# Where ScalarE's two last exponentials stand among the copies of the transposed weights

## Chip, cores and metric

The kernel runs on one core of a Trainium2 chip. The metric is the device time of one execution in microseconds (us). The core has a matrix engine (TensorE, PE in the profile, with its weight loads listed apart as PEld), VectorE (DVE), ScalarE (ACT), GpSimd (POOL) and a queue engine (SP). Each engine works through its own list of instructions in order; semaphores order the engines against each other.

## What is computed

Two layers on x of 2 x 512 tokens x 256 features, all in float32. Layer 0 is a state-space scan and a mixture of eight experts. Layer 1 is causal attention with 32 query heads and 8 key/value heads of 64, gated by a network of signs. Only the attention of layer 1 matters here:

```python
q = (h @ Wq.T)...; k = (h @ Wk.T)...; v = (h @ Wv.T)...   # 32, 8 and 8 heads of 64
q, k = apply_rope(q), apply_rope(k)
logits = einsum('bhqd,bhkd->bhqk', q, k) * scale
logits = where(causal, logits, finfo.min)
attn = softmax(logits)
out = einsum('bhqk,bhkd->bhqd', attn, v)
return out.reshape(b, s, H * HD) @ Wo.T
```

## The kernel before

Everything ahead of the attention (layer 0 and the first projections of layer 1) is not touched. The attention is one hand-written order of work under a manual schedule: the loop `for n, (b, c) in enumerate(work)` has 32 iterations, n = 0 to 31, one for each pair of heads (16 pairs in each of two batches). The two heads of a pair are numbered hh = 0 and 1. The 512 queries are four tiles of 128, i = 0 to 3; because of the causal mask tile i meets (i + 1) x 128 keys, so that the last tile (`last`, i = 3) is 128x512.

The loop is staggered: iteration n scores pair n, and transposes and applies the weights of pair n - 1, which are finished by then. In iteration n each engine finds this order:

- TensorE: `scores` (L1213, 32 matmuls); the query projection of pair n + 1 (`projected`, L1145, 4 matmuls); 20 transposes of the weights of pair n - 1 (`transposed`, L1252) into six banks of PSUM, three for each head; in iterations 1 to 17 a piece of other work from a list (`others`: key and value projections, gates); then `values` (L1264, 16 matmuls), which multiplies the transposed weights with v.
- VectorE: `greatest` (L1226), which masks the scores, moves them from PSUM to the tile `pr` and finds the maximum `nmax`; in between `kept` (L1409, L1412), which stores the result of `values`; the rotation of the next query (L1135 to L1140) with the reciprocal of the sums of tiles 0 to 2 in its middle (L1428); then the reciprocal of the sums of tile 3 of both heads (`den3`, L1450) and the normalisation of tile 3 of head 0 (L1240).
- ScalarE: `exponentials` (L1232) of tiles 0 to 2, two heads each, in place in `pr`, with the row sum as a second result; then the six copies (L1253) that bring the transposed weights of pair n - 1 from PSUM to the tile `pt`, two of 128x512 and four of 128x384; the two exponentials of tile 3, 128x512 each; and the normalisation of tile 3 of head 1 (L1238).
- GpSimd: the normalisation of tiles 0 to 2 (L1240), six instructions.

The order on ScalarE between the copies and the last two exponentials is written out in the loop. `transposed(pts, pr, n)` does bank n of both heads: TensorE's transposes and ScalarE's two copies. Before, it is: bank 0, exponential of head 0, banks 1 and 2, exponential of head 1.

PSUM is eight banks handed out in turn (`bank`), `pt` has three buffers for the two of each iteration. `values` waits for each copy by itself: its matmuls go through key tiles j = 0 to 3, for j = 0 from the copies of bank 0, for j = 1 from bank 1, for j = 2 and 3 from bank 2. After iteration 31 the kernel sums the output projection (`summed`, L1272) for what is finished, transposes and copies pair 31 with no exponential among the copies, applies its values and ends.

Of the kernel before, what the change touches and what calls it, by code (L numbers as in the profile page):

```python
# [51 lines left out]
def fused_kernel(  # L52
# [41 lines left out]
    def bank(width=512):  # L94

        if not later:
            return bank_b()
        i = turns[0] % 8
        turns[0] += 1
        written[i] = max(written[i], width)  # L100
        return later[i]
# [1075 lines left out]
    def query(b, c, between=None):  # L1177
        q = aw.tile([P, T], F32, tag="q", name=f"q{b}_{c}")
        rotated(q, projected(w_q, c, b), 1.0, f"q{b}_{c}", between)
        return q  # L1180

    last = TPB - 1

    def scores(b, c, q):

        m = c // 4
        w = dict(  # L1190
            nmax=[aw.tile([P, TPB], F32, tag=f"nmax{hh}", name=f"nmax{b}_{c}_{hh}")
                  for hh in range(2)],

            den=aw.tile([P, 2, last], F32, tag="den0", name=f"den{b}_{c}_0"),
            den3=aw.tile([P, 2], F32, tag="den1", name=f"den{b}_{c}_1"),
            pr=[aw.tile([P, PACK], F32, tag=f"pr{hh}", name=f"pr{b}_{c}_{hh}")
                for hh in range(2)],
            ps={})
        for tiles in ((0, 1), (2,), (3,)):
            ready = written[turns[0] % 8], written[(turns[0] + 1) % 8]  # L1200
            pss = [bank(sum(i + 1 for i in tiles) * P) for _ in range(2)]
            for i in tiles:
                a = sum((k + 1) * P for k in tiles if k < i)
                cols = slice(a, a + (i + 1) * P)
                w["ps"][i] = [p[:, cols] for p in pss]
                for part in range(2):
                    to = slice(part * HD, (part + 1) * HD)
                    for hh in range(2):
                        half = slice(hh * HD, (hh + 1) * HD)
                        n = 2 * i + (part ^ (i & 1))  # L1210

                        full = (n + 1) * HD if ready[hh] >= cols.stop else (i + 1) * P
                        PE.matmul(pss[hh][to, a : a + full], lhsT=q[half, n * HD : (n + 1) * HD],  # L1213
                                  rhs=kT[b][half, m, :full], start=True, stop=True)
        return w

    def span(i):
        return slice(row_at[i], row_at[i] + (i + 1) * P)

    def sum_of(w, i, hh):  # L1220
        return w["den3"][:, hh : hh + 1] if i == last else w["den"][:, hh, i : i + 1]

    def greatest(w, i):

        for hh in range(2):
            V.tensor_tensor_reduce(w["pr"][hh][:, span(i)], w["ps"][i][hh],  # L1226
                                   cmask[:, i & 1, T - (i + 1) * P :], -1.0, 3.0e38, ALU.add, ALU.min,
                                   w["nmax"][hh][:, i : i + 1])

    def exponentials(w, i, hh):  # L1230
        x = w["pr"][hh][:, span(i)]
        S.activation(x, x, AF.Exp, scale=-1.0, bias=w["nmax"][hh][:, i : i + 1],  # L1232
                     accum_out=sum_of(w, i, hh))

    def normalised(w, i, hh, eng):
        x = w["pr"][hh][:, span(i)]
        if eng is S:
            S.mul(x, x, sum_of(w, i, hh))  # L1238
        else:
            eng.tensor_scalar(x, x, sum_of(w, i, hh), None, ALU.mult)  # L1240

    def transposes_begun(b, c):
        return [late.tile([P, PACK], F32, tag="pt", name=f"pt{b}_{c}_{hh}", bufs=3)
                for hh in range(2)]

    def transposed(pts, pr, n):
        for hh in range(2):
            ps = bank(widths[n])
            for (j, i), (bk, col) in place.items():
                if bk == n:  # L1250
                    at = row_at[i] + j * P
                    PE.transpose(ps[:, col : col + P], pr[hh][:, at : at + P], ident)  # L1252
            S.copy(pts[hh][:, bank_at[n] : bank_at[n] + widths[n]], ps[:, : widths[n]])  # L1253

    def values(b, c, pts):

        pv = bank()
        for j in range(TPB):
            bk, col = place[j, j]
            at = bank_at[bk] + col  # L1260
            w = T - j * P
            for hh in range(2):
                g = 2 * (c // 4) + hh
                PE.matmul(pv[hh * HD : (hh + 1) * HD, j * P :],  # L1264
                          lhsT=v_sb[b][:, j, g * HD : (g + 1) * HD],
                          rhs=pts[hh][:, at : at + w],
                          start=(j == 0), stop=(j == TPB - 1))
        return pv

    def summed(ps, b, i, pairs):  # L1270
        for c in pairs:
            PE.matmul(ps[:, :C], lhsT=oTs[b][:, c, i * P : (i + 1) * P],  # L1272
                      rhs=made["w_o"][c // 8][:, c % 8, :],
                      start=(c == 0), stop=(c == PAIRS - 1))
# [126 lines left out]
    def kept(b, c, pv):  # L1401
        if b not in oTs:
            oTs[b] = late.tile([P, PAIRS, T], F32, tag="oT", name=f"oT{b}")
        def halves(ap):
            return ap.rearrange("p (u s r q) -> p s r u q", s=2, r=2, q=HD)


        o, pv = oTs[b][:, c, :], pv[:, :]
        V.tensor_copy(o.rearrange("p (u s q) -> p s u q", s=2, q=P)[:, 0],  # L1409
                      pv.rearrange("p (u s q) -> p s u q", s=2, q=P)[:, 0])  # L1410
        for r in range(2):
            V.tensor_copy(halves(o)[:, 1, r], halves(pv)[:, 1, 1 - r])  # L1412

    with tc.manual_schedule():
        prev = done = None
        for n, (b, c) in enumerate(work):
            w = scores(b, c, nextq)
            for i in range(TPB):
                greatest(w, i)
                if i == 1 and done is not None:  # L1420
                    kept(*done)
                    done = None
                if i < last:
                    for hh in range(2):
                        exponentials(w, i, hh)

            def between():
                V.reciprocal(w["den"], w["den"])  # L1428

            if n + 1 < len(work):  # L1430
                nextq = query(*work[n + 1], between)
            else:
                between()
            for hh in range(2):
                for i in range(last):
                    normalised(w, i, hh, G)
            if prev is not None:
                pb, pc, pw = prev
                pts = transposes_begun(pb, pc)
                transposed(pts, pw["pr"], 0)  # L1440
                exponentials(w, last, 0)
                transposed(pts, pw["pr"], 1)
                transposed(pts, pw["pr"], 2)
                exponentials(w, last, 1)
            else:
                exponentials(w, last, 0)
                exponentials(w, last, 1)
            if others:
                others.pop(0)()
            V.reciprocal(w["den3"], w["den3"])  # L1450
            normalised(w, last, 0, V)
            normalised(w, last, 1, S)
            if prev is not None:
                done = (pb, pc, values(pb, pc, pts))
            prev = (b, c, w)
            if done is not None and done[1] == PAIRS - 1:
                kept(*done)
                done = None
                for i in range(TPB):
                    ps = bank(C)  # L1460
                    summed(ps, pb, i, range(PAIRS))
                    ended(ps, pb, i)

        kept(*done)
        pss = [bank(C) for _ in range(2)]
        for i in range(2):
            summed(pss[i], b, i, range(PAIRS - 1))
        pts = transposes_begun(b, c)
        for k in range(3):
            transposed(pts, w["pr"], k)  # L1470
        turns[0] += 2
        kept(b, c, values(b, c, pts))
        for i in range(2):
            summed(pss[i], b, i, range(PAIRS - 1, PAIRS))
            ended(pss[i], b, i)
        for i in range(2, TPB):
            ps = bank(C)
            summed(ps, b, i, range(PAIRS))
            ended(ps, b, i)
# [87 lines left out]
```

## Time and profile before

| what | value |
|---|---|
| median of the runs before | 644.58 us (three runs: 639.34, 644.58, 645.81) |
| the profiled execution, device time | 638.66 us |
| its span from the first to the last instruction | 636.9 us |
| TensorE's granted clock in it | 0.996 |
| busy: PE, DVE, ACT, POOL | 608.4, 430.3, 357.4, 276.8 us |
| the attention loop within the span | 256 to about 600 us |
| the output projection of batch 0 inside it | 440 to 468 us |
| iterations 19 to 30, from one to the next | 8.70 to 8.72 us |

All times inside the program come from the profiled execution and are counted from the first instruction of its span. "Idle before" an instruction is the time in which its engine did nothing ahead of it, and the arrow names what ended it. Matmuls overlap: a matmul's own duration in the profile is longer than the distance to the next one, so the time of a phase of matmuls is read from the first start to the last end, and a phase takes its first start to the next phase's first start of the engine.

### The profile page before, as it was taken

The page shows a single profiled execution, that of the slowest core. Times are in us where ns is not written, and L with a number is a line of the kernel's source. Part 1 is how long each engine was busy: PE and PEld are TensorE (multiplying, and loading weights), DVE is VectorE, ACT ScalarE, POOL GpSimd, SP SyncE. Part 2 cuts the span into 40 slices and gives each one's busy share as a digit, 9 for nine tenths or more (in the row PEclk, how much of TensorE's full clock was granted, in tenths as well). Part 3 has the DMA queues.
Part 4 walks back from the last instruction along what each step waited for, and adds up shares of the span by engine and source line. Part 5 has one row for each costly group of instructions (what it writes and reads, how often), then busy time and mean ns, then how long its engine had stood idle before and what let it go on. Part 6 is the DMA issues. An engine that isn't in the chain of part 4 may idle for free.

```text
span 636.9 us, 10937 instructions
## 1 busy us (share of the span) xinstructions
PE 608.4 (96%) x3818; PEld 411.2 (65%) x3818; DVE 430.3 (68%) x1375; ACT 357.4 (56%) x917; POOL 276.8 (43%) x309
## 2 busy tenths in 40 slices
PE   4999999999999998998899999899999999999997
PEld 2568888777577764454556565557866656666676
DVE  7587654564442257899989987996159888888411
ACT  2534333142331413868889877787058888898610
POOL 3021220264557312465566556365025776666600
PEclk9999999999999998999999999999999999999999
DMA  7710440555767344000000000040000000000000
GB/s 228 269 33 18 174 162 21 204 197 208 245 210 243 117 173 142 2 2 2 2 2 0 1 2 2 2 133 2 16 17 2 2 2 1 1 2 1 2 9 25
DMA packets 24988, 45.75 MB, mean 72 GB/s; under 512 B 2621, under 2 KB 12607, under 8 KB 24928
## 3 DMA queue, kind: packets, MB, share of 16 engines
q1 hardware_dynamic: 19024, 29.66, 13.5%
q0 software_dynamic: 4512, 13.77, 6.9%
q10 hardware_dynamic: 1392, 1.57, 0.7%
q8 instruction: 32, 0.52, 0.3%
q14 instruction: 28, 0.23, 0.1%
HBM read 40.80 MB, written 4.33 MB: 71 GB/s over the span
## 4 chain that ended last, share of the span: by engine, by line
PE 46%; DVE 14%; DMA 2%; issue 1%; POOL 1%; ACT 0%; ACTq 0%; DVEq 0%; POOLq 0%
PE bank L1264 9%; PE bank L1272 9%; PE bank L1252 8%; PE bank L1145 8%; PE bank L1213 8%; DVE pr L1226 5%; PE bank L1162 1%; DMA chosen<-o,dest 1%; PE bank L1124 1%; DVE sw_q L1135 1%; DVE xn L236 1%; DVE q L1136 1%; POOL pr L1240 1%; PE bank_b L1145 1%; DVE oT L1412 1%
## 5 line engine op out<-in xcount | busy, mean ns | idle before, releaser
L1240 POOL TENSOR_SCALAR pr<-pr,den 128x128 f32<-128x128 f32 (+2 forms) x192 | 193.1, 1021 | 154.2 <-DVE den L1428 121.0
L1232 ACT ACTIVATE pr<-pr,nmax 128x128 f32<-128x128 f32 (+3 forms) x256 | 142.7, 558 | 18.4 <-DVE nmax L1226 17.0
L1226 DVE CUSTOM_DVE_ANT_0 pr<-bank,cmask 128x128 f32<-128x128 f32 (+3 forms) x256 | 109.7, 484 | 14.5 <-PE bank L1213 11.9
L1253 ACT COPY pt<-bank 128x384 f32<-128x384 f32 (+1 forms) x192 | 84.8, 518 | 13.1 <-PE bank L1252 13.1
L1252 PEld LDWEIGHTS bank<-ident,pr 128*128 128x128 f32 x640 | 71.2, 141 | 24.7 <-issue 18.2
L1264 PE MATMUL bank<-pt,v 128*64 128x256 f32 (+3 forms) x512 | 82.5, 443 | 0.8 <-ACT pt L1253 0.8
L1252 PE MATMUL bank<-ident,pr 128*128 128x128 f32 x640 | 75.7, 273 | 6.0 <-DVE oT L1412 5.7
L633 PE MATMUL bank_a<-xgT,w 128*128 128x256 f32 x352 | 79.5, 379 | 0.0
L633 PEld LDWEIGHTS bank_a<-xgT,w 128*128 128x128 f32 x352 | 65.5, 190 | 9.2 <-issue 1.0
L1264 PEld LDWEIGHTS bank<-pt,v 128*64 128x64 f32 x512 | 39.3, 136 | 48.6 <-ACT pt L1253 22.3
L1213 PE MATMUL bank<-kT,q 64*64 64x128 f32 (+7 forms) x1024 | 69.8, 410 | 0.7 <-ACT v L1164 0.7
L1145 PE MATMUL bank<-x1T,w_q 128*128 128x512 f32 x124 | 61.5, 618 | 0.0
L1272 PE MATMUL bank<-w_o,oT 128*128 128x256 f32 x256 | 56.1, 380 | 0.6 <-DVE oT L1409 0.6
L1272 PEld LDWEIGHTS bank<-w_o,oT 128*128 128x128 f32 x256 | 48.3, 190 | 7.7 <-DVE oT L1409 0.8
L1232 ACT ACTIVATION_READ_ACCUMULATOR pr<-pr,nmax 128x1 f32 x256 | 49.1, 192 | 0.0
L1213 PEld LDWEIGHTS bank<-kT,q 64*64 64x64 f32 x1024 | 38.0, 133 | 14.3 <-issue 5.1
L596 POOL DMA_INDIRECT chosen<-o,dest x16 | 16.1, 1007 | 70.5 <-ACT o L595 35.4
L584 POOL DMA_INDIRECT piece<-in_moe,wrow x36 | 37.2, 1033 | 18.5 <-issue 9.4
L1145 PEld LDWEIGHTS bank<-x1T,w_q 128*128 128x128 f32 x124 | 21.0, 189 | 36.9 <-issue 27.7
L658 PE MATMUL bank_a<-wp,hid 128*128 128x256 f32 x192 | 43.0, 380 | 0.0
L584 POOL DMA_INDIRECT xg<-rows,tok x16 | 16.8, 1050 | 56.5 <-DVE res L909 32.3
L658 PEld LDWEIGHTS bank_a<-wp,hid 128*128 128x128 f32 x192 | 35.9, 190 | 5.8 <-issue 1.3
(275 smaller groups left out, 801.7 us busy)
## 6 DMA issues: line engine op xcount, KB each, us to landing
w<-in_moe SPq DMA_DIRECT2D x8, 1024.0 KB, 7.2
wp<-in_moe SPq DMA_DIRECT2D x8, 768.0 KB, 4.8
w<-in_moe SPq DMA_DIRECT2D x8, 384.0 KB, 7.6
w_q<-in_wq SPq DMA_DIRECT2D x2, 1024.0 KB, 9.1
w_o<-in_wo SPq DMA_DIRECT2D x2, 1024.0 KB, 7.0
rows<-xn SPq DMA_DIRECT2D x4, 256.0 KB, 2.2
xn<-chosen SPq DMA_DIRECT2D x4, 256.0 KB, 2.9
out_x<-y SPq DMA_DIRECT2D x8, 128.0 KB, 1.7
```

Source lines behind the costliest of these rows:

```text
L584: G.indirect_dma_start(out=buf, out_offset=None, in_=src[:, :], in_offset=bass.IndirectOffsetOnAxis(ap=at, axis=0), bounds_check=src.shape ...
L633: PE.matmul(ps[:, i * OWN : (i + 1) * OWN], lhsT=w[:, a : a + P], rhs=xgT[:, k * OWN : (k + 1) * OWN], start=(k == 0), stop=(k == KC - 1))
L658: PE.matmul(ps[:, :C], lhsT=hid[j // 2][:, a : a + P], rhs=wp[:, j * C : (j + 1) * C], start=(j == 0), stop=(j == 5))
L1145: PE.matmul(ps, lhsT=w[:, k, n * P : (n + 1) * P], rhs=x1T[:, k, batch(b)], start=(k == 0), stop=(k == KC - 1))
L1213: PE.matmul(pss[hh][to, a : a + full], lhsT=q[half, n * HD : (n + 1) * HD], rhs=kT[b][half, m, :full], start=True, stop=True)
L1226: V.tensor_tensor_reduce(w["pr"][hh][:, span(i)], w["ps"][i][hh], cmask[:, i & 1, T - (i + 1) * P :], -1.0, 3.0e38, ALU.add, ALU.min, w["n ...
L1232: S.activation(x, x, AF.Exp, scale=-1.0, bias=w["nmax"][hh][:, i : i + 1], accum_out=sum_of(w, i, hh))
L1240: eng.tensor_scalar(x, x, sum_of(w, i, hh), None, ALU.mult)
L1252: PE.transpose(ps[:, col : col + P], pr[hh][:, at : at + P], ident)
L1253: S.copy(pts[hh][:, bank_at[n] : bank_at[n] + widths[n]], ps[:, : widths[n]])
L1264: PE.matmul(pv[hh * HD : (hh + 1) * HD, j * P :], lhsT=v_sb[b][:, j, g * HD : (g + 1) * HD], rhs=pts[hh][:, at : at + w], start=(j == 0), ...
L1272: PE.matmul(ps[:, :C], lhsT=oTs[b][:, c, i * P : (i + 1) * P], rhs=made["w_o"][c // 8][:, c % 8, :], start=(c == 0), stop=(c == PAIRS - 1))
```

## The change

```diff
             if prev is not None:
                 pb, pc, pw = prev
                 pts = transposes_begun(pb, pc)
-                transposed(pts, pw["pr"], 0)
-                exponentials(w, last, 0)
-                transposed(pts, pw["pr"], 1)
-                transposed(pts, pw["pr"], 2)
-                exponentials(w, last, 1)
-            else:
-                exponentials(w, last, 0)
-                exponentials(w, last, 1)
+                for k in range(3):
+                    transposed(pts, pw["pr"], k)
+            for hh in range(2):
+                exponentials(w, last, hh)
             if others:
                 others.pop(0)()
```

In iterations 1 to 31 the exponential of tile 3 of head 0 moves on ScalarE from behind the second copy to behind the sixth. Iteration 0, which has no pair to transpose, keeps its order. As built, the lists of TensorE, VectorE, GpSimd and the queues are the same instructions in the same order as before (source lines behind the edit move up by four). On ScalarE 31 exponentials change place; the wait of each for VectorE's maximum goes, in 30 of the iterations, into an instruction of its own that stands ahead of the sixth copy.

## The prediction

> **What bounds the kernel now.** I read the page for the busy engine, then the chain that ended last for the stage, then the waits and timelines inside one iteration of that stage.
>
> ```profile
> PE 608.4 (96%) x3818; PEld 411.2 (65%) x3818; DVE 430.3 (68%) x1375; ACT 357.4 (56%) x917; POOL 276.8 (43%) x309
> ...
> L1253 ACT COPY pt<-bank 128x384 f32<-128x384 f32 (+1 forms) x192 | 84.8, 518 | 13.1 <-PE bank L1252 13.1
> ...
> L1264 PEld LDWEIGHTS bank<-pt,v 128*64 128x64 f32 x512 | 39.3, 136 | 48.6 <-ACT pt L1253 22.3
> ```
>
> TensorE is busy 96% of the span, but its ends are modelled, so small holes hide in that. The last line shows one: the weight loads of the values phase were held 22.3 us in total by ScalarE's copies. The chain says where that is on the path. From iteration 18 (482 us) to iteration 29 it never leaves TensorE; four pieces of iteration 22, and the values of pair 31 after the loop:
>
> ```profile
> 516.80 2.18 PE bank L1252 x20
> 518.99 2.51 PE bank L1264 x15
> 521.50 2.10 PE bank L1213 x28
> 523.60 1.91 PE bank L1145 x4
> ...
> 615.17 2.33 PE bank L1264 x16
> ```
>
> Transposes, values, scores, query: 8.70 us. The values phase takes 2.51 us in the loop and 2.33 us at the end for the same 16 matmuls. The timelines of TensorE (start, duration) agree:
>
> ```profile
> 518.92 2.58 PE L1264 MATMUL bank<-pt,v 128*64 128x512 f32 x16
> ...
> 615.10 2.38 PE L1264 MATMUL bank<-pt,v 128*64 128x512 f32 x16
> ```
>
> ScalarE in the same iteration, then its copies for pair 31, where no exponential stands among them:
>
> ```profile
> 517.31 1.05 ACT L1253 COPY pt<-bank 128x512 f32<-128x512 f32 x2
> 518.26 0.72 ACT L1232 ACTIVATE pr<-pr,nmax 128x512 f32<-128x512 f32 x1
> 518.88 0.19 ACT L1232 ACTIVATION_READ_ACCUMULATOR pr<-pr,nmax 128x1 f32 x1
> 518.97 1.61 ACT L1253 COPY pt<-bank 128x384 f32<-128x384 f32 x4
> 520.44 0.76 ACT L1232 ACTIVATE pr<-pr,nmax 128x512 f32<-128x512 f32 x1
> 521.06 0.23 ACT L1232 ACTIVATION_READ_ACCUMULATOR pr<-pr,nmax 128x1 f32 x1
> 521.52 0.72 ACT L1238 ACTIVATE pr<-pr,den 128x512 f32<-128x512 f32 x1 [0.23 <-DVE den L1450]
> ```
>
> ```profile
> 613.46 2.61 ACT L1253 COPY pt<-bank 128x512 f32<-128x512 f32 x6 [12.87 <-PE bank L1252]
> ```
>
> In the loop the last copy ends at 518.97 + 1.61 = 520.58, 1.66 us after the values began; at the end of the kernel at 613.46 + 2.61 = 616.07, 0.97 us after. That is the whole difference between a held phase and a free one. VectorE, last, shows who waits for the second exponential:
>
> ```profile
> 521.32 0.17 DVE L1450 RECIPROCAL den<-den 128x2 f32<-128x2 f32 x1 [0.89 <-ACT pr L1232]
> 521.52 0.54 DVE L1240 TENSOR_SCALAR pr<-pr,den 128x512 f32<-128x512 f32 x1
> 522.36 0.29 DVE L1226 CUSTOM_DVE_ANT_0 pr<-bank,cmask 128x128 f32<-128x128 f32 x1 [0.30 <-PE bank L1213]
> ```
>
> **The change, part by part.**
>
> Copies 3 to 6 go earlier. Nothing is added to ScalarE but one wait for each iteration; the work is the same. In iteration 22 the exponential of head 0 starts at 518.26 and the next copy at 518.97, so the copies gain 0.71 us. Their data must be there: TensorE's timeline ends the last transposes of the four banks at 518.01, 518.33, 518.66 and 518.99, and the copies (0.36 to 0.37 us from one start to the next in this row) would start at 518.25, 518.61, 518.98 and 519.35: 0.24 to 0.36 us of margin. The last then ends at about 519.87, 0.95 us after the values began, as for pair 31 (0.97), whose phase was free. So the phase falls from 2.51 to 2.31 us on the chain.
>
> Whether the modelled ends of transposes can be trusted decides that margin. For pair 31 ScalarE was idle, the last transpose of the first bank is modelled to end at 613.43, and the copy starts at 613.46. So the model is right within 0.03 us. The Trainium skill (Perfetto Trace Analysis, Tensor Engine Instruction) says that the profiler computes a matmul's end and that the semaphore comes later. By that rule alone the copies could be late and the gain smaller; the row above leaves at most 0.03 us, so the sum keeps the full gain.
>
> How many times: the chain has 12 values phases in iterations 18 to 29, of 2.50 to 2.55 us, 30.12 us together; at the free 2.31 us they are 27.72. Gain 2.40 us. Iteration 30's phase is held too (0.20 us), but the chain passes there through VectorE and GpSimd (normalising pair 30 until 594.8), so it counts nothing. Iteration 31 has no query projection and its transposes wait for GpSimd: its copies begin only at 595.66, its values run from 596.51 to 599.84, 3.33 us instead of 2.38, and TensorE follows directly with 13.15 us of output projection. After the change its sixth copy ends about 0.72 us earlier, near 598.2, and 0.2 us earlier still because iteration 30's values end sooner. I take 0.9 us, between 0.7 (the copies' gain alone) and 0.95 (all that was held).
>
> The exponential of head 0 goes later, by four copies, about 1.46 us. Its reader is the reciprocal L1450, which needs both heads. So the question is when the second exponential ends. The pair of iteration 0, adjacent already, starts at 260.78 and 261.49: 0.71 us, as much as the exponential costs between copies. I take 0 for the end of the second one. Bounds: 0.1 us sooner (one overlap more between neighbours: copies and exponentials overlap by 0.09 to 0.14) and 0.73 us later (a whole exponential exposed).
>
> The wait that moves ahead of the sixth copy, 30 times. It asks for head 0's maximum of tile 3, which VectorE has written by 517.15; the copy starts at 519.35, so it holds nothing. Queued behind it are that copy and both exponentials. The nearest row is ScalarE's own semaphore instructions at L1232: 32 of them, 17 ns at the median, 38 at most. Between 0 and 30 x 0.038 = 1.1 us; I take 0, since 17 ns fit into the copies' margin. No DMA or queue is moved past.
>
> Who takes over. With 8.50 us an iteration, VectorE still waits at `greatest`: 0.30 - 0.20 = 0.10 us remain. ScalarE is idle 0.23, 0.52 and 0.18 us in an iteration. GpSimd ends pair 22's normalisation at 525.14 while the transpose that needs it starts at 526.00; 0.86 shrinks to 0.66. So TensorE stays the bound.
>
> Iterations 1 to 17: in 1, 3, 5, 6 and 9 to 17 other matmuls stand between the transposes and the values (2.37 us, free already). In 2, 4, 7 and 8 the values take 3.45, 3.55, 2.65 and 2.71 us, an excess of 2.88 us together, but VectorE has no idle time there: in iteration 2 it comes to L1450 at 286.77 and to the next `greatest` at 287.34, back to back, long after ScalarE's exponential (284.7). I take 0, with 2.9 us as the other end.
>
> Sum: -2.40 - 0.9 = -3.3 us. Against the profiled execution (span 636.9, device time 638.66) that is 635.4 us. Its time lies 5.92 us below the median of the runs shown, 644.58; I carry the difference over, which gives 641.3 us, or 0.5% less.
>
> **The rivals.**
>
> A. VectorE becomes the bound and it ends slower. If the second exponential ends later by d, L1450 waits longer, and the next `greatest` is late by what exceeds 0.10 us at the shorter iteration, 0.30 us at today's. From d = 0.30 on, the change loses. At the bound of 0.73 us an iteration is 0.43 us longer than today, over 13 iterations 5.6 us, less 0.9 in iteration 31: 644.58 + 4.7 = 649.3. For it: VectorE waits 0.89 us at exactly this place. Against: the adjacent pair of iteration 0 costs 0.71 us, and the copies have their margin.
>
> B. The hole is not ScalarE's order. It repeats evenly on the engine that should be full, so buffers could be short: `pt` has three, PSUM eight banks. Then nothing changes: 644.58. Against: pair 31 uses the same buffers and banks, and its phase is free. The Trainium skill (Perfetto Trace Analysis, Optimization Strategy) reads the same gap over a stretch as a possible sign of too little SBUF or PSUM for the next tile. By that rule the time stays; the trace does not agree, since the wait ends with the copies.
>
> C. The early iterations gain as well: 2.9 us more and iteration 30's 0.2, 644.58 - 6.4 = 638.2. Against: VectorE's rows there have no gap.
>
> D. Half of it: GpSimd or VectorE stops the shorter iteration after 0.10 us. 12 x 0.10 + 0.9 = 2.1 us, 642.5. For it: only 0.10 us remains at `greatest`. Against: GpSimd's 0.66 us and ScalarE's idle time.
>
> **How the numbers follow.** The forecast has 0.66, D 0.12, A 0.08, B 0.07, C 0.07. The likeliest gives 641.3. The three runs before lie between 639.34 and 645.81, which is the bigger uncertainty: the forecast's own range is those less 3.3, 636.0 to 642.5, and the lower execution is as good a start as the median. B's and D's times reach 645, C's from the lowest run 632.9. I give 634.5 to 645.8, leaving out most of A and the far end of C. A measurement of this kernel tells about 1% from no change (6.4 us). The forecast, B and D are all within it; C stands on the edge; A reaches it only with d above 0.85 us, past its bound, or with a slow draw on top. With the runs' scatter: faster by over 1% 0.13, within 1% 0.81, slower by over 1% 0.06.
>
> **What would show it.** In iterations 19 to 29 of the changed kernel: an iteration of 8.50 us instead of 8.70; values phases of about 2.37 us in TensorE's timeline and 2.31 on the chain; the weight loads' wait for `pt` nearly gone from this stretch; six copies in one row with no idle time, the two exponentials 0.71 us apart; the reciprocal of `den3` no later after the scores than today (8.60 us after the iteration's first score); VectorE's wait at `greatest` down to 0.1 us. In iteration 31 values of 2.4 to 2.6 us. Up to 440 us nothing but scatter. I am wrong if the copies wait for transposes, if the reciprocal comes over 0.1 us later, or if the first half of the loop moves.

## The result and the profile after

| | before | changed |
|---|---|---|
| median of the timed runs | 643.64 us (639.14 to 648.12, 20 runs) | 639.03 us (635.08 to 642.76, 20 runs) |
| profiled execution, device time | 638.66 us | 642.76 us |
| its span | 636.9 us | 641.0 us |
| first score of the attention, from the span's start | 256.44 us | 263.87 us |
| from the first score to the end of the span | 380.50 us | 377.18 us |

The changed kernel takes 0.9936 of the time before (95% interval 0.991 to 0.9961). 641.3 us was forecast, 639.03 us was measured.

The profiled execution of the changed kernel is longer than that of the kernel before, and the table shows why: all that the change touches comes after the first score (the first matmul of L1213), and the part ahead of it, which is the same in both, took 7.43 us more in this execution. So everything below is read from the first score on, and this piece is called the stretch. It repeats to within 0.1 us: two kernels whose values phases ran as before had 380.58 and 380.59 us, against 380.50, and a second profile of the changed kernel had 377.12, against 377.18. (One pair of kernels repeats less well, in its early iterations; that stands with kept_on_scalar.) The time to the first score lay between 252.71 and 263.87 us over the 14 profiles of this study, whatever the kernel.

Lines of the page of the changed kernel, the same three as before:

```profile
PE 605.1 (94%) x3818; PEld 407.8 (64%) x3818; DVE 430.6 (67%) x1375; ACT 357.5 (56%) x917; POOL 277.2 (43%) x309
...
L1253 ACT COPY pt<-bank 128x384 f32<-128x384 f32 (+1 forms) x192 | 82.3, 523 | 12.4 <-PE bank L1252 12.4
...
L1264 PEld LDWEIGHTS bank<-pt,v 128*64 128x64 f32 x512 | 35.3, 136 | 47.0 <-issue 21.9
```

ScalarE's copies are no longer named as what ends the idle time of the weight loads. But the idle time itself fell only from 48.6 to 47.0 us; the section on the prediction comes back to that.

The chain of the changed kernel in iteration 22, and the values of pair 30 in iteration 31:

```profile
523.42 2.18 PE bank L1252 x20
525.60 2.30 PE bank L1264 x16
527.90 2.10 PE bank L1213 x28
530.00 1.91 PE bank L1145 x4
...
601.59 2.35 PE bank L1264 x16
```

The four pieces sum to 8.49 us; from one iteration to the next it is 8.50. Only the values phase differs from before: 2.30 instead of 2.51. TensorE's timeline of the same two phases:

```profile
525.53 2.37 PE L1264 MATMUL bank<-pt,v 128*64 128x512 f32 x16
...
601.51 2.42 PE L1264 MATMUL bank<-pt,v 128*64 128x512 f32 x16
```

2.37 us is the length of a free phase, one that waits for no copy, and iteration 31 has 2.42 us where it had 3.33. ScalarE's timeline of iteration 22:

```profile
523.92 2.57 ACT L1253 COPY pt<-bank 128x512 f32<-128x512 f32 x6
526.35 0.76 ACT L1232 ACTIVATE pr<-pr,nmax 128x512 f32<-128x512 f32 x1
526.98 0.23 ACT L1232 ACTIVATION_READ_ACCUMULATOR pr<-pr,nmax 128x1 f32 x1
527.07 0.75 ACT L1232 ACTIVATE pr<-pr,nmax 128x512 f32<-128x512 f32 x1
```

The six copies stand in one unbroken row and end at 526.49, 0.96 us after the values began (1.66 before). The second exponential starts 0.72 us after the first. VectorE's timeline:

```profile
527.94 0.17 DVE L1446 RECIPROCAL den<-den 128x2 f32<-128x2 f32 x1 [0.89 <-ACT pr L1232]
528.14 0.54 DVE L1240 TENSOR_SCALAR pr<-pr,den 128x512 f32<-128x512 f32 x1
528.77 0.29 DVE L1226 CUSTOM_DVE_ANT_0 pr<-bank,cmask 128x128 f32<-128x128 f32 x1
```

The reciprocal comes 8.61 us after the iteration's first score (8.60 before). Behind the normalisation 0.09 us remain until `greatest` (528.14 + 0.54 to 528.77), where 0.30 us had been.

### The profile page after: what moved, and what is told of

Same layout as the page of the kernel before. It is cut to its first block, busy times and chain, and to the rows that moved or that the text cites. A ratio compares the mean times of both kernels' runs of the same rounds, so it can differ in the third digit from the quotient of the medians.

```text
span 641.0 us, 10967 instructions
## 1 busy us (share of the span) xinstructions
PE 605.1 (94%) x3818; PEld 407.8 (64%) x3818; DVE 430.6 (67%) x1375; ACT 357.5 (56%) x917; POOL 277.2 (43%) x309
## 4 chain that ended last, share of the span: by engine, by line
PE 48%; DVE 13%; DMA 1%; issue 1%; POOL 1%; ACT 0%; ACTq 0%; DVEq 0%; POOLq 0%
PE bank L1264 9%; PE bank L1272 9%; PE bank L1213 8%; PE bank L1252 8%; PE bank L1145 8%; DVE pr L1226 4%; PE bank L1162 2%; DMA y<-chosen 1%; PE bank L1124 1%; DVE sw_q L1135 1%; PE bank_b L1145 1%; POOL pr L1240 1%; DVE q L1136 1%; DVE x_sb L1092 1%; DVE xn L236 1%
## 5 line engine op out<-in xcount | busy, mean ns | idle before, releaser
L1240 POOL TENSOR_SCALAR pr<-pr,den 128x128 f32<-128x128 f32 (+2 forms) x192 | 193.4, 1024 | 151.6 <-DVE den L1428 120.1
L1253 ACT COPY pt<-bank 128x384 f32<-128x384 f32 (+1 forms) x192 | 82.3, 523 | 12.4 <-PE bank L1252 12.4
L1264 PE MATMUL bank<-pt,v 128*64 128x128 f32 (+3 forms) x512 | 76.9, 439 | 0.8 <-ACT pt L1253 0.8
L1213 PE MATMUL bank<-kT,q 64*64 64x128 f32 (+7 forms) x1024 | 69.8, 410 | 0.7 <-ACT v L1164 0.7
L1264 PEld LDWEIGHTS bank<-pt,v 128*64 128x64 f32 x512 | 35.3, 136 | 47.0 <-issue 21.9
L1213 PEld LDWEIGHTS bank<-kT,q 64*64 64x64 f32 x1024 | 38.0, 133 | 14.3 <-issue 5.5
```

The costliest lines, as they stand in the source:

```text
L1264: PE.matmul(pv[hh * HD : (hh + 1) * HD, j * P :], lhsT=v_sb[b][:, j, g * HD : (g + 1) * HD], rhs=pts[hh][:, at : at + w], start=(j == 0), ...
```

## The experiments

The theory at the outset: the end of the sixth copy alone sets the length of the values phase, and the end of the second exponential, by way of VectorE, is the next limit. The rivals: every copy that is delayed costs its share; buffers; ScalarE's idle time takes up whatever is added; and the change in the early iterations counts too. The diffs are shortened to the lines that matter. Those of only_31, only_18_30, behind_bank_1 and before_four_pt are written against the kernel before, the later ones against the changed kernel. All readings in one table, in us, each from one profile ("it." is the iteration's first score):

| kernel | first score | stretch | first score to it. 17 | it. 17 to 30 | it. 30 to end |
|---|---|---|---|---|---|
| before | 256.44 | 380.50 | 211.19 | 114.73 | 54.57 |
| changed | 263.87 | 377.18 | 211.24 | 112.25 | 53.69 |
| only_31 | 255.36 | 379.89 | 211.20 | 114.81 | 53.89 |
| only_18_30 | 253.92 | 377.82 | 211.19 | 112.25 | 54.38 |
| behind_bank_1 | 255.32 | 380.59 | 211.20 | 114.81 | 54.58 |
| before_four_pt | 254.58 | 380.58 | 211.19 | 114.81 | 54.58 |
| both_first | 256.74 | 391.43 | 211.35 | 123.74 | 56.35 |
| extra_copy | 257.19 | 382.62 | 210.67 | 116.86 | 55.09 |
| extra_copies | 252.71 | 388.36 | 211.89 | 120.69 | 55.78 |
| kept_on_scalar | 257.14 | 381.28 | 215.35 | 112.25 | 53.68 |
| tail_vector | 257.48 | 377.17 | 211.19 | 112.25 | 53.73 |
| both_additions | 254.64 | 379.63 | 213.64 | 112.25 | 53.73 |
| tail_order | 261.34 | 376.37 | 211.26 | 112.25 | 52.86 |
| changed_again | 259.40 | 377.12 | 211.20 | 112.25 | 53.67 |

**The change in iteration 31 alone, and in iterations 18 to 30 alone** (only_31, only_18_30). Elsewhere the order is that of before.

```diff
+            late_both = n == 31            # only_18_30: 18 <= n <= 30
             transposed(pts, pw["pr"], 0)
-            exponentials(w, last, 0)
+            if not late_both:
+                exponentials(w, last, 0)
             transposed(pts, pw["pr"], 1)
             transposed(pts, pw["pr"], 2)
+            if late_both:
+                exponentials(w, last, 0)
             exponentials(w, last, 1)
```

> The new order in iteration 31 alone. Measure: the time from the first score of the loop to the end of the span, which leaves out the scatter of layer 0 (before 380.50 us, changed kernel 377.18). My theory (the end of the sixth copy holds TensorE's values phase, and each place on the chain counts by itself): iterations 18 to 30 stay at 8.70 us, the values of iteration 31 fall from 3.33 us to 2.5 to 2.6 (the last 0.2 us of the gain there needs the shorter iteration 30), stretch 379.7 to 379.8. Rival, the gain comes as a whole from making the two exponentials neighbours in each iteration: about 1/31 of 3.3 us, stretch 380.4.

> The new order in iterations 18 to 30 alone. My theory: iterations of 8.50 us there as in the changed kernel, iteration 31's values near 3.1 us (its copies start 0.2 us earlier but keep the exponential among them), iterations 1 to 17 as before; stretch from the first score to the end 377.8 to 378.0 us. Rival, the early iterations carry part of the gain: more of the 3.3 us is missing than the 0.7 us of iteration 31, stretch above 378.3.

TensorE's timeline of only_31, iterations 30 and 31:

```profile
587.56 2.58 PE L1264 MATMUL bank<-pt,v 128*64 128x512 f32 x16
...
595.52 2.64 PE L1264 MATMUL bank<-pt,v 128*64 128x512 f32 x16
```

The first line is still the held phase, the second has lost 0.69 of its 3.33 us. The last column of the table is 0.68 us shorter (0.69 against the two repeats); the stretch is 0.61 us shorter than before, or 0.69 and 0.70 than the repeats. The phase and the stretch (379.89 us) both came out a little above what was expected. In only_18_30 iterations take 8.50 us, the stretch loses 2.68 us (2.48 up to iteration 30 and 0.19 behind it), and iteration 31's values take 3.12: 0.2 us less, although its order is the old one, because the phase ahead of it ends sooner. The parts add up to 3.3 to 3.4 us, by the baseline taken for only_31 (0.61 + 2.68 = 3.29, 0.69 + 2.68 = 3.37), where the whole change gives 3.33 to 3.38. With iterations 1 to 17 left as before, only_31 and only_18_30 lose nothing: there the change is worth nothing, and the rival about the early iterations falls.

**The exponential of head 0 in the middle** (behind_bank_1): behind the fourth copy, not the second.

```diff
             transposed(pts, pw["pr"], 0)
-            exponentials(w, last, 0)
             transposed(pts, pw["pr"], 1)
+            exponentials(w, last, 0)
             transposed(pts, pw["pr"], 2)
             exponentials(w, last, 1)
```

> The exponential of head 0 stands behind the copies of bank 1, between copies 4 and 5, in all iterations. Copies 3 and 4 come 0.71 us earlier, copies 5 and 6 start where they did before. My theory, only the sixth copy's end decides, since TensorE reaches the last key tiles when that copy ends: iterations 19 to 30 stay at 8.68 to 8.71 us and the values phase at about 2.58 us; stretch 380.3 to 380.5 us, as before. Rival, each copy that comes earlier gives its share: two of four copies moved, about half of the gain, 8.60 us an iteration and a stretch near 379.

ScalarE's timeline and then TensorE's:

```profile
516.23 1.81 ACT L1253 COPY pt<-bank 128x512 f32<-128x512 f32 x4
517.92 0.74 ACT L1232 ACTIVATE pr<-pr,nmax 128x512 f32<-128x512 f32 x1
518.54 0.21 ACT L1232 ACTIVATION_READ_ACCUMULATOR pr<-pr,nmax 128x1 f32 x1
518.64 0.86 ACT L1253 COPY pt<-bank 128x384 f32<-128x384 f32 x2
```

```profile
517.84 2.58 PE L1264 MATMUL bank<-pt,v 128*64 128x512 f32 x16
```

Copies 3 and 4 come as early as in the changed kernel, copies 5 and 6 as late as before (the last ends at 519.50, 1.66 us after the values began), and the phase is 2.58 us: nothing is gained, and 380.59 us is the stretch of before. Only the last bank's copies count; the rival that every copy costs its share falls.

All 14 traces together give the rule that is behind this, for these 16 matmuls and six copies. Of their 448 values phases 307 are free. In 139 of the 141 longer ones the phase ends 0.92 to 0.93 us after the last copy, whatever the order (the two others are those of iteration 31 in tail_vector and both_additions, where VectorE makes three of the copies). So a last copy that ends by 2.37 - 0.92 = 1.45 us after the phase's start costs nothing; in the free phases it ends by 1.39 at the latest. Before, it ended at 1.66, 0.21 us too late, which is the gain of an iteration. Of the 0.71 us by which the reorder advances the copies only these 0.21 us count, and 0.48 us are left over (0.97 in the changed kernel).

**One more buffer, the old order** (before_four_pt).

```diff
-        return [late.tile([P, PACK], F32, tag="pt", name=f"pt{b}_{c}_{hh}", bufs=3)
+        return [late.tile([P, PACK], F32, tag="pt", name=f"pt{b}_{c}_{hh}", bufs=4)
```

> The kernel before, with four buffers for the transposed weights instead of three. Rival of the prediction, the even hole comes from too few buffers: the values phase falls to about 2.37 us and the iteration to 8.50. My theory, the order on ScalarE makes it: 8.70 us an iteration, values 2.58 us, stretch from the first score to the end 380.5 us as before.

```profile
517.08 2.58 PE L1264 MATMUL bank<-pt,v 128*64 128x512 f32 x16
...
525.79 1.49 PE L1264 MATMUL bank<-pt,v 128*64 128x512 f32 x6
```

TensorE's timeline in that kernel (the second phase is cut off by the window): the phases begin 8.71 us apart and take 2.58 us, as before. `pt` was not short. The Trainium skill (Perfetto Trace Analysis, Optimization Strategy) lets an even gap on the engine that should be full point to too few buffers; here the gap was as even as that and came from an instruction's place on another engine. More banks of PSUM weren't tried, since the kernel already hands out all eight. The reorder empties the banks sooner as well, so that it brings the free length does not exclude them by itself; against them stands that the held phases end a fixed 0.92 us after the last copy.

**Both exponentials ahead of the copies** (both_first), to see whether the copies' lateness passes on in full.

```diff
+            for hh in range(2):
+                exponentials(w, last, hh)
             for k in range(3):
                 transposed(pts, pw["pr"], k)
-            for hh in range(2):
-                exponentials(w, last, hh)
```

> The opposite order: both exponentials of the last tile ahead of all six copies. The sixth copy then ends another 0.71 us later than before, at 521.30 in the frame of iteration 22 of the kernel before, where it ended at 520.58. My theory: the last key tiles of the values phase start when that copy ends, so the next scores come 0.55 to 0.75 us later than before: 9.25 to 9.45 us an iteration in 18 to 30, values phase of about 3.1 to 3.3 us; the reciprocal of den3 is early and no longer waits for ScalarE in a way that matters; stretch from the first score to the end 387 to 390 us. Rival, ScalarE's reciprocal is the binding wait (VectorE waits 0.89 us for it): an earlier reciprocal shortens the iteration below 8.70 us or leaves it.

Two iterations in TensorE's timeline:

```profile
532.25 2.87 PE L1264 MATMUL bank<-pt,v 128*64 128x512 f32 x16 [0.36 <-ACT pt L1253]
...
541.67 2.86 PE L1264 MATMUL bank<-pt,v 128*64 128x512 f32 x16 [0.36 <-ACT pt L1253]
```

9.42 us an iteration, 0.71 more than before: one exponential passes on in full. It splits in two, however: from the first transpose to the first matmul of the values it takes 2.70 us instead of 2.28 (0.36 of it is the wait in the brackets), and from there to the next score 2.80 instead of 2.51. The expectation had put all of it inside the phase. The stretch, 391.43 us, missed its range from above (10.9 us lost instead of 6.5 to 9.5): iterations 17 to 30 lose 9.0 us, and the tail another 1.8.

**A copy more between the sixth copy and the exponentials** (extra_copy, extra_copies): it moves the exponentials later and leaves the copies alone, so it prices the other side. The added work goes to a tile that nobody reads.

```diff
             for k in range(3):
                 transposed(pts, pw["pr"], k)
+            for _ in range(1):             # extra_copies: 2
+                S.copy(scr, pts[0][:, bank_at[1] : bank_at[1] + widths[1]])
```

> The changed kernel with one more ScalarE instruction in each iteration, a 128x384 copy from pt to a scratch tile that nobody reads, between the sixth copy and the two exponentials, so the reciprocal of den3 comes later by about 0.37 us and nothing else is touched. The changed kernel's VectorE has 0.09 us idle ahead of its first maximum, and up to 0.17 us if back-to-back overlap is counted. My theory: beyond that slack every bit counts, 8.50 + 0.37 - 0.17 = 8.70 us an iteration (8.65 to 8.80) in 18 to 30, stretch 379.5 to 381. Rival, ScalarE's own idle time (0.23 + 0.31 us in an iteration) takes it: 8.50 us, stretch 377.2.

> The same with two such copies, about 0.74 us. My theory: 8.50 + 0.74 - 0.17 = 9.07 us an iteration (9.0 to 9.2) in 18 to 30, stretch 384 to 386 us, so that the step from one to two copies costs its whole 0.37 us in each iteration. Rival with ScalarE's own slack of 0.54 us: 8.70 us, stretch 379.8.

ScalarE's timeline of extra_copy, then VectorE's:

```profile
538.92 0.56 ACT L1445 COPY scr<-pt 128x384 f32<-128x384 f32 x1
539.34 0.76 ACT L1232 ACTIVATE pr<-pr,nmax 128x512 f32<-128x512 f32 x1
```

```profile
540.93 0.17 DVE L1450 RECIPROCAL den<-den 128x2 f32<-128x2 f32 x1 [1.31 <-ACT pr L1232]
541.13 0.78 DVE L1240 TENSOR_SCALAR pr<-pr,den 128x512 f32<-128x512 f32 x1
541.83 0.27 DVE L1226 CUSTOM_DVE_ANT_0 pr<-bank,cmask 128x128 f32<-128x128 f32 x1
```

The exponentials start d = 0.42 us later (538.92 to 539.34), and VectorE's wait for them grows from 0.89 to 1.31, by the same 0.42. Nothing of it is absorbed on ScalarE. The limit can be worked out from the kernel before: `greatest` starts at 513.66, and after the exponentials and the normalisation (521.52, 0.54 us) the next could start at 521.98, since neighbours on VectorE overlap by 0.08 us (541.13 + 0.78 against 541.83 above). That is 8.32 us. So the loop through VectorE and ScalarE takes 8.32 + d, and TensorE's 8.50 us leaves 0.18. For extra_copy that makes 8.74 us, 8.96 were measured; the rest, 0.22, is about what the normalisation takes longer, 0.78 us here instead of 0.54. ScalarE's timeline of extra_copies, and VectorE's:

```profile
547.06 1.10 ACT L1445 COPY scr<-pt 128x384 f32<-128x384 f32 x2
548.06 0.72 ACT L1232 ACTIVATE pr<-pr,nmax 128x512 f32<-128x512 f32 x1
```

```profile
549.82 0.56 DVE L1240 TENSOR_SCALAR pr<-pr,den 128x512 f32<-128x512 f32 x1
```

Here d = 1.00 us, the normalisation is 0.56, and 8.32 + 1.00 + 0.02 = 9.34 stands against 9.31 measured. The rival that ScalarE's idle time takes up what is added falls. Both sizes had been expected too low (8.65 to 8.80 and 9.0 to 9.2), and the stretches with them.

**Head 1's copies of the last iteration on VectorE** (tail_vector). In iteration 30 VectorE also normalises tile 2 of head 1.

```diff
-    normalised(w, i, hh, G)
+    normalised(w, i, hh, V if n == 30 and hh and i == 2 else G)
...
-    S.copy(...)
+    (V.tensor_copy if n == 31 and hh else S.copy)(...)
```

> The changed kernel, with VectorE's idle time at the end of the loop used: in iteration 30 VectorE instead of GpSimd normalises tile 2 of head 1 (GpSimd's last of six, 1.24 us, which the transposes of iteration 31 wait for), and in iteration 31 VectorE instead of ScalarE makes the copies of head 1. My theory: the chain there is GpSimd's normalisation, then ScalarE's copies; GpSimd's end comes 1.2 us sooner and ScalarE has three copies instead of six ahead of the values, so the stretch from iteration 30's first score to the end falls from 53.7 us by 0.6 to 0.9 us, to 52.8 to 53.1; everything ahead of it stays (iterations of 8.50 us). Rival: ScalarE's exponentials of tile 2 hold the first copy all the same, and nothing is gained.

The chain of that kernel:

```profile
592.80 1.31 ACT pr L1232 x4
594.11 0.48 ACT pt L1253
594.63 2.93 PE bank L1265 x14
```

Nothing gained (53.73 us from iteration 30's first score, where 52.8 to 53.1 was expected): GpSimd is off the chain, but ScalarE's exponentials of tile 2 now hold the first copy, which ends only 0.04 us before the values can start (594.59 and 594.63). VectorE in turn begins its three copies only at 594.48, behind its last maxima, and the values take 2.93 us instead of 2.42. One wait took the place of another.

**Copies of results on ScalarE in the early iterations** (kept_on_scalar), since VectorE bounds those.

```diff
-    kept(*done)                        # V.tensor_copy
+    kept(*done, S.copy)                # n <= 14, behind the exponentials of tile 1
```

> The changed kernel, with the three copies of each stored result (0.75 us of VectorE) moved to ScalarE in iterations 2 to 14. The changed kernel left iterations 1 to 17 at 211.2 us, as before. My theory: that is because VectorE bounds about six of these (iterations 2, 3, 4, 5, 8, 14), and ScalarE has over 0.7 us to spare there; so the move saves 0.5 to 0.75 us in each, 3 to 4.5 us from the first score to iteration 17: 206.7 to 208.2 us. Rival: ScalarE's copies and exponentials come 0.9 us later and hold TensorE's values or the reciprocal, as in the run with the exponentials first: no gain, or a loss of up to 3 us.

The chain of that kernel in iteration 4, and a piece of iteration 5:

```profile
301.27 1.86 ACT pr L1232 x8
303.13 0.26 ACT oT L1409
303.38 0.32 ACT oT L1412 x2
303.71 1.22 ACT pr L1232 x4
304.92 0.02 issue
304.95 0.19 DVE den L1431
...
314.26 0.33 ACT oT L1412 x2
314.60 0.14 issue
314.73 3.45 PE bank L1252 x20
```

My theory fell: the time to iteration 17 is 4.1 us longer (215.35 us), where it was to gain 3 to 4.5. The copies delay the exponentials behind them on ScalarE, and VectorE's reciprocal waits for those; relief of the bound engine came back to it as a wait. In iteration 5 TensorE's transposes wait for the copies too, and the 20 of them take 3.45 us at a granted clock of 0.50, against 2.37 us at 1.00 in iteration 4. both_additions below has the same order up to iteration 17 and needs 213.64 us; there the transposes run at 0.50 in iteration 4 instead, and the two kernels part in iterations 4 and 5 alone. So 2.4 us of the loss repeat, and 1.7 don't.

**Both of these** (both_additions).

> Both of these together on top of the change, timed. My theory: against the changed kernel 0.6 to 0.9 us at the end and 3 to 4.5 us in iterations 2 to 14, so 372 to 373.5 us from the first score to the end (changed kernel 377.2, before 380.5), and 1.1 to 1.4% less than before in the runs' times. Rival as for the two alone: no better than the changed kernel, 0.6% less than before.

638.31 us against 637.03 for the kernel before on that chip: ratio 1.0014 (0.9991 to 1.0037), where 1.1 to 1.4% less was expected. The stretch is 379.63 us instead of 372 to 373.5: the gain of the change, less 2.45 us lost in the early iterations.

**Another order in the tail** (tail_order), and the changed kernel beside it (changed_again). In iteration 31 the copies also go ahead of tile 2's exponentials, and in iteration 30 VectorE normalises tile 2 of head 1.

```diff
             # n == 31
             exponentials of tiles 0 and 1
+            for k in range(3):
+                transposed(pts, pw["pr"], k)
             exponentials of tile 2
-            for k in range(3):
-                transposed(pts, pw["pr"], k)
             exponentials(w, last, 0); exponentials(w, last, 1)
```

> The changed kernel; in iteration 31 ScalarE makes the six copies ahead of the exponentials of tile 2 too, and in iteration 30 VectorE instead of GpSimd normalises tile 2 of head 1. The run with VectorE's copies gained nothing, because the first copy still began 4.59 us after the iteration's first score, when ScalarE had done the exponentials of tile 2, and VectorE's copies could not begin sooner either. My theory: the copies begin when the tile-1 exponentials end, 3.1 us after the first score, the values end about 1.2 us sooner, and the stretch from iteration 30's first score to the end falls from 53.7 to 52.4 to 52.7 us; from the first score of the loop to the end 375.9 to 376.2 us (changed kernel 377.2, before 380.5). Rival: the later exponentials of pair 31 are missing at its transposes, and the end comes no sooner. Against before: 0.6 to 0.8% less in the runs' times.

> The changed kernel once more, beside the kernel before on one chip. My theory: 377.2 us from the first score to the end (before 380.5), so 0.5% less in the runs' times, and what the first measurement showed beyond that (0.64%) is the scatter of layer 0. Rival: the gain is bigger than the attention shows, because layer 0 is faster as well; then 0.65% or more again.

TensorE's timeline of tail_order:

```profile
596.38 1.94 PE L1252 MATMUL bank<-ident,pr 128*128 128x128 f32 x16 [0.26 <-DVE oT L1412]
598.24 2.37 PE L1264 MATMUL bank<-pt,v 128*64 128x512 f32 x16
```

The values of the last iteration are free (2.37 us), and the tail is 52.86 us instead of 53.67 to 53.69; 52.4 to 52.7 was expected. The first line accounts for 0.26 us: with GpSimd and ScalarE out of the way, the transposes wait that long for VectorE, which has yet to empty a bank (`oT`, L1412). The changed kernel has this wait too, ahead of a longer one for GpSimd. On one chip tail_order had 636.86 us, ratio to the kernel before 0.9906 (0.9868 to 0.9944), and the changed kernel 639.08 us, ratio 0.9938 (0.9897 to 0.9978); its 0.62% lies between the 0.5% expected and the rival's 0.65%, and the interval holds both. The two intervals overlap; that tail_order is the fastest version rests on the stretch, 376.37 against 377.12 us.

## Why the prediction was right, step by step

- **The held phase, -2.40 us.** Right. Iterations 17 to 30 went from 114.73 to 112.25 us, 2.48 us less, an iteration takes 8.50 us, and the phase on the chain 2.30. That the last copy's end is the cause was argued from a comparison with pair 31; behind_bank_1 and the held phases of all 14 traces show it. The prediction had the free length right by comparison, and did not work out that only 0.21 of the copies' 0.71 us was needed.
- **Iteration 31, -0.9 us.** Right in its size and in both its parts: 54.57 to 53.69 is 0.88 us, of which only_31 shows 0.69 for the copies and only_18_30 shows 0.19 for the earlier phase ahead (54.57 to 54.38).
- **The pair of exponentials ends no later, 0.** Right: they start 0.72 us apart, the second one 7.74 us after the first score against 7.72 before.
- **The extra wait, 0.** Right: the profile of the changed kernel has 31 semaphore instructions at L1253 where there was one, each of 17 ns, and no idle time in the row of six copies. In iteration 22 the wait is over at 525.33, and the sixth copy starts at 525.98.
- **Iterations 1 to 17, 0.** Right: 211.19 and 211.24 us, although the values of iterations 2, 4, 7 and 8 did become shorter (2.76, 2.85, 2.38 and 2.38 us). VectorE took that time back: the first score of iteration 3 comes 27.71 us after that of iteration 0 instead of 28.40, but iteration 3's first `greatest` starts at 30.92, and at 30.90 before. So single iterations moved by up to 0.7 us and back, and "nothing but scatter" holds for their sum only.
- **The sum, -3.3 us.** Right: the stretch lost 3.33 us, and 3.38 in the second profile. By the timed runs 0.9936 of 643.64 us is 4.1 us less (2.5 to 5.8); 3.3 us is a ratio of 0.9949 and lies in that interval, and in that of the second measurement. Whether anything beyond 3.3 us is there can't be told from the times, and the stretch shows none.
- **The forecast 641.3 us against 639.03.** 0.9 us of the 2.3 is the start: the median before was 644.58 over three runs and 643.64 over twenty. The rest is of the size of the scatter ahead of the first score.
- **The rivals.** Buffers (B): no change with four `pt`. Early iterations (C): no gain there. Half of it (D): the full 8.50 us was reached. VectorE as the bound (A) was a true danger, not met: with d = 0 it doesn't bite, but the added copies show its slope: 9.31 - 8.32 = 0.99 us for d = 1.00, and 0.64 for d = 0.42, of which 0.24 is the longer normalisation. Its threshold, 0.10 us, was a little low, because it left out the overlap of VectorE's neighbours: 8.50 - 8.32 = 0.18, and at the old iteration 8.71 - 8.32 = 0.39 instead of 0.30.
- **One sign was wrong.** The weight loads' wait for `pt` was to be nearly gone. The waits of TensorE's weight loads in iterations 18 to 31, before (480 to 600 us), then changed (488 to 606 us); the columns are us in total, times, longest:

```profile
PEld bank L1264 <- ACT pt L1253: 8.9, 30, 0.9
```

```profile
PEld bank L1264 <- ACT pt L1253: 6.9, 31, 0.3
```

The total fell by 2.0 us, no more, and 6.9 us remain in a kernel whose phases are free. This row counts the time of the weight loads' own track: in the changed kernel's iteration 22 waits of 0.17 and 0.28 us fall into the values phase, which takes the free 2.37 us all the same. So the 22.3 us quoted from the page were never a measure of the hole; the phase lengths (12 times 0.2 us) were, and the sum went by them. What did change is the longest wait, from 0.9 to 0.3 us (the 0.9 is iteration 31's; in iteration 22 it is 0.38 before and 0.28 after).

## What to carry to other kernels

Where a chain stays on one engine and one phase in it is longer than the same phase elsewhere in the same profile, the difference times its count is what a reorder can bring; then find which single instruction ends last ahead of the phase and by how much it is too late, because here moving the others brought nothing, and moving it by more than 0.21 us no more. Before an instruction is moved behind others, work out the loop that runs through its reader, for that loop can become the bound: here it left 0.18 us in 8.50. And when a change is confined to one part of the program, measure from a fixed instruction ahead of that part: 3.3 us was plain in the stretch in a single profile, while the profiled execution as a whole had become 4.1 us longer.

## What the runs showed of the hardware

- **Nearly all of the scatter lies ahead of the attention.** The first score came between 252.71 and 263.87 us over 14 profiles; behind it, before, behind_bank_1 and before_four_pt agree within 0.1 us, and so do the two profiles of the changed kernel. What in layer 0 scatters wasn't tried.
- **A granted clock of 0.50 can move 1.7 us within the attention.** kept_on_scalar and both_additions have the same order up to iteration 17 and reach it after 215.35 and 213.64 us. TensorE waits 2.19 us ahead of iteration 5's transposes in the first and 3.13 us ahead of iteration 4's in the second, and runs them at 0.50 (316 to 318 and 302 to 304 us). The first kernel waits 3.13 us in iteration 4 as well and runs at 1.00 behind it, so the wait alone doesn't decide; what does stays open.
- **VectorE's normalisation of 128x512 isn't of one length.** 0.54 us in iteration 22 of the changed kernel, 0.78 in extra_copy, 0.56 in extra_copies, the same instruction on the same shape. In iterations 2 and 14 no GpSimd instruction runs beside it, and it takes 0.49 us; in the three cases above one does (L1240). The Trainium skill (SBUF — State Buffer, Who interferes with whom) says that VectorE in some modes, which this kind of instruction can enter, and GpSimd take a shared pair of ports by turns, and that the later of the two is blocked. A wait for a whole GpSimd instruction doesn't show here: in iteration 22 of the changed kernel, VectorE's 0.54 us lie inside a single one of 1.24 us. A shorter wait may be part of the longer times, but no run here separates it: it was seen, not tested.
- **The modelled ends of TensorE's transposes were good enough for a margin of 0.24 us.** In iteration 22 of the changed kernel they put the data of copies 3 to 6 0.26 to 0.38 us ahead of their starts (0.24 to 0.36 was worked out beforehand), and that of the first two 0.07 and 0.10 us; all six ran with no idle time.
